# Mixing gated low-rank adapters on eight tiles of the array, and first adapter products in pairs

## The chip, the cores and the metric

The kernel runs on one core of a Trainium2 chip. The core has five instruction streams: TensorE (PE; its weight loads are listed as PEld), VectorE (DVE), ScalarE (ACT), GpSimd (POOL) and SyncE (SP), which here only issues DMAs. Each stream executes its instructions in order and waits on semaphores for the others. The metric is the device time of one execution in microseconds (us); a profiled execution is taken apart from the timed runs and lists every instruction with its start and duration.

## The reference

The input `x` holds 64 rows of 64 channels and 1024 positions. A grouped convolution with nine taps runs along the positions; a condition vector and a bias are added per row and channel. The result goes through a 1024 x 1024 matrix with a bias and through two low-rank adapters ("loras") of rank 32: a shared one, and one that is a gated mixture of sixteen. `x` is added at the end.

```python
out = conv(x, weight, padding=4, groups=4) + (c @ c_weight.T)[:, :, None] + bias   # 64 x 64 x 1024
base_out = out @ kernel + bias
A_eff = einsum("bn,nri->bri", gate, lora_A)        # 8 batches, 16 adapters, rank 32
B_eff = einsum("bn,nor->bor", gate, lora_B)
delta = B_eff (A_eff out)  +  lora_B_shared (lora_A_shared out)
return x + base_out + delta
```

The gate holds one row of sixteen numbers for each of eight batches, and the mixture is computed for any gate.

## The kernel before, in words

**Precision and shape of the work.** Products are made from operands split into a high and a low part: ScalarE rounds the high part (`hi_of`, L264), VectorE or GpSimd subtracts it to get the low part (`lo_of`, L269), and three matmuls (high by high, high by low, low by high) make one product. The 64 rows are worked on as 16 pairs of 256 matrix rows each; eight batches hold two pairs each (`BP = 2`).

**Stages of a pair.** Its input comes in four groups (`xload`). From pair 3 on, a group's convolution is made of two parts: `convo` (the odd positions, three matmuls of 256 columns, fed by `xohi`, `xolo`) and `convd` (the differences, six matmuls, fed by `xdiff`, `xdhi`, `xdlo`). `evmid` (L359) takes the first out of PSUM, on ScalarE in four pieces or on VectorE in one, `evac` (L368) adds it to the second, and `turned` (L382) transposes on VectorE into the tiles `z`. The matrix product follows Strassen's scheme with seven products `prod p j` of twelve 512-column matmuls (L582), whose left sides are blocks of `z` or sums of them (`asum`, `yhi`, `ylo`). Pair 0 is done by the plain scheme (`plain`, L572), while the weights are still being loaded (`wload`), have the shared adapter folded in (`fmm`, `fadd`), and are summed and split (`wsum`, `whi`, `wlo`). Results are put together by `keep`, `xsum`, `ysum`, `radd`, `yadd`, and `total` adds the accumulator to the residual row block (`rload`), which `store` writes out.

**Adapters.** `gmask` (L508) builds the stationary matrix of a mix from the gate. `lload w i` loads raw adapters, sixteen pieces of 256 KB. `mix w j` (L523) multiplies two of them by the gate matrix, `mixout` (L531) copies the PSUM bank out on ScalarE, `mixput` (L538) writes it to a DRAM tile `eff`, from which `aload b` (L548) and `bload b h` (L552) fetch a batch's mixed A and B. `lora p` (L597) is the first adapter product of a pair: sixteen matmuls of 128 columns with a stationary of 32 columns, which go to four column tiles of the array in turn and land in the PSUM tile `axp`. `axlow`, `axsum`, `axhi`, `axlo` sum and split its result; `delta p b` (L655) is the second adapter product, one matmul per block, added to the block's accumulator before `total`. The stationary of `delta` carries two rows of ones; `biput` (L744) writes the high and low part of the bias to the two matching rows of the other operand, `bst`.

**What sets the order.** The string `ORDER` (from L50), called the listing here, names each step with its arguments; a last `v`, `p` or `a` chooses VectorE, GpSimd or ScalarE. The steps are emitted in this order (L748), and each of the five streams is then held to it (L757). Where a step falls against steps of another stream is left to the semaphores. Buffers are few: four `z` tiles (two pairs), five PSUM banks for products and mixes (`pmm`), two for the convolution, four residual blocks.

Of the kernel before, what the change touches and what calls it, by code (L numbers as in the profile page):

```python
# [10 lines left out]
ALU = mybir.AluOpType  # L11
# [39 lines left out]
small 1, warm, twload 1, busy 29, twload 0, cwload, gload, ctload, cwide, cmul, thi 2, small 0, thi 0, tlo 0 v,  # L51
xload 0 0, xhi 0 0, tlo 2 p, xload 0 1, xlo 0 0 v, conv 0 0, twsum v, xhi 0 1, xlo 0 1 v, conv 0 1, sbload 1,
sbhi 1, csum, evac 0 0 v, turned 0 0, xload 0 2, xhi 0 2, xload 0 3, saload 0, sblo 1 p, xlo 0 2 p, evac 0 1 v,
turned 0 1, saload 1, gmask, xhi 0 3, conv 0 2, xlo 0 3 p, sahi 1, conv 0 3, sahi 0, salo 0 v, fmm 0 1,
sbload 0, sbhi 0, fmm 1 1, wload 1 0, evac 0 2 a, xload 1 0, sblo 0 v, fmm 1 0, salo 1 v, xload 1 1, xhi 1 0,
xhi 1 1, xlo 1 1 p, xlo 1 0 v, turned 0 2, yhi 0 0, ylo 0 0 p, wload 0 1, fadd 0 1, evac 0 3 a, fadd 1 0,
conv 1 0, whi 7 0, fmm 4 0, turned 0 3, xload 1 2, xhi 1 2, wlo 7 0 v, fmm 3 0, wload 1 1, conv 1 1, fadd 1 1,
wload 4 0, fmm 0 0, whi 0 1, wload 0 0, fadd 0 0, evac 1 0 a, plain 0 1 0, fadd 4 0, xlo 1 2 p, turned 1 0,
whi 0 0, wlo 0 1 p, fmm 2 1, fmm 2 0, yhi 0 7, evac 1 1 a, conv 1 2, fmm 5 0, wload 2 1, wload 2 0, fadd 2 0,
wlo 0 0 p, plain 0 0 0, xload 1 3, fadd 2 1, wload 5 0, xhi 1 3, fmm 4 1, xlo 1 3 p, plain 0 0 1, whi 0 2,  # L60
ylo 0 7 v, fadd 5 0, plain 0 3 0, whi 7 1, yhi 0 4, wload 3 0, fadd 3 0, whi 0 3, wload 5 1, fmm 3 1, conv 1 3,
turned 1 1, wlo 7 1 v, wload 3 1, xload 2 0, plain 0 1 1, fadd 3 1, whi 7 2, evac 1 2 v, wlo 7 2 p, wload 4 1,
wlo 0 3 p, wlo 0 2 v, lload 0 6, plain 0 2 0, whi 7 3, plain 0 3 1, fadd 4 1, wload 7 1, turned 1 2, whi 1 1,
plain 0 1 2, lload 0 7, xhi 2 0, plain 0 0 2, ylo 0 4 v, plain 0 3 2, xlo 2 0 v, plain 0 2 1, fmm 5 1,
evac 1 3 a, xload 3 0, wlo 7 3 v, plain 0 2 2, turned 1 3, whi 1 0, yhi 0 1, ylo 0 1 v, fadd 5 1, whi 6 1,
conv 2 0, wload 7 0, thi 1, xdiff 3 0 0 v, wload 6 0, evac 2 0 a, lload 1 5, wlo 1 0 p, fmm 7 0, fadd 7 0,
plain 0 2 3, plain 0 0 3, fmm 6 0, lload 0 2, plain 0 3 3, plain 0 1 3, fadd 6 0, lload 0 5, whi 6 0, asum 1 2,
yhi 1 2, lload 0 0, yhi 1 0, plain 0 0 4, plain 0 2 4, wsum 2 2 v, whi 2 2, lload 1 1, wlo 1 1 p, plain 0 0 5,
fmm 6 1, tlo 1 v, plain 0 2 5, rload 0 2, wlo 6 0 v, wsum 2 1 v, wsum 2 3 v, whi 1 2, wlo 1 2 v, plain 0 1 4,
whi 2 1, asum 1 3, whi 1 3, wlo 1 3 p, xload 2 2, wload 6 1, fadd 6 1, xload 2 1, whi 6 2, lload 0 1, xhi 2 2,  # L70
plain 0 3 4, lload 0 4, plain 0 2 6, lload 1 0, lload 0 3, wsum 2 0 v, fmm 7 1, plain 0 2 7, xload 2 3,
plain 0 0 6, fadd 7 1, whi 6 3, total 0 2, lload 1 6, mix 0 0, mixout 0 0 a, wlo 6 2 v, xhi 2 1, wlo 6 3 v,
wlo 6 1 v, wsum 3 2 v, xlo 2 2 v, mix 0 3, mixout 0 3 a, mix 0 2, mixout 0 2 a, wsum 3 0 v, wsum 5 0 v,
mixput 0 0, whi 2 3, mix 0 1, wsum 3 1 v, mix 1 0, mixput 0 3, mixout 0 1 a, xdiff 3 0 1 p, wsum 4 0 v,
conv 2 2, wlo 2 2 v, whi 2 0, wlo 2 0 v, ylo 1 2 v, plain 0 1 5, wsum 5 1 v, rload 0 0, wsum 5 2 v, wsum 4 2 v,
xlo 2 1 v, plain 0 0 7, mixput 0 1, ylo 1 0 p, mixput 0 2, wlo 2 1 v, prod 1 0, plain 0 1 6, wsum 3 3 v,
wsum 5 3 v, rload 0 1, plain 0 3 5, wsum 4 3 v, bihi, whi 3 2, keep 1 0, plain 0 1 7, lload 1 3, wsum 4 1 v,
plain 0 3 6, mixout 1 0 a, lload 1 7, mix 1 3, aload 0, whi 5 3, yhi 1 3, rload 0 3, lload 1 2, ylo 1 3 v,
mixout 1 3 a, total 0 1, lora 0, mix 1 1, turned 2 0, lora 1, whi 5 0, bilo, xohi 3 0, lload 1 4, mix 1 2,
whi 4 2, wlo 4 2 v, mixout 1 1 a, xolo 3 0 v, whi 3 0, wlo 3 0 v, wlo 3 2 v, yhi 1 1, ylo 1 1 v, mixout 1 2 a,  # L80
asum 1 5, total 0 0, whi 4 1, conv 2 1, axlow 1, axsum 1, xload 3 2, wlo 4 1 p, wlo 2 3 v, whi 4 0,
plain 0 3 7, axlow 0, axsum 0, mixput 1 0, mixput 1 3, wlo 4 0 v, xhi 2 3, xlo 2 3 v, wlo 5 3 v, axhi 1,
prod 1 1, biput 0, axlo 1, whi 3 3, asum 1 6, yhi 1 6, wlo 3 3 v, mixput 1 1, evac 2 1 a, turned 2 1, aload 1,
mixput 1 2, total 0 3, evac 2 2 v, turned 2 2, bload 0 0, whi 3 1, axhi 0, prod 1 2, keep 1 2, conv 2 3,
bhi 0 0, biput 1, yhi 2 0, evac 2 3 a, blo 0 0 v, axlo 0, yhi 1 4, bload 0 1, wlo 3 1 p, prod 1 3, ylo 2 0 v,
delta 0 0 1, total 0 0 1, bhi 0 1, blo 0 1 v, ylo 1 6 p, prod 1 6, whi 4 3, delta 0 3 1, wlo 4 3 v, store 0 0,
ylo 1 4 p, turned 2 3, delta 0 2 1, total 0 3 1, xdhi 3 0, convo 3 0, yhi 1 5, whi 5 1, ylo 1 5 v, xdlo 3 0 v,
delta 1 0, total 0 2 1, xload 3 1, keep 1 3, prod 1 4, evmid 3 0 a, store 0 3, xohi 3 1, xdiff 3 1 0 v,
xdiff 3 1 1 p, wlo 5 1 p, delta 0 1 1, total 0 1 1, wlo 5 0 v, xolo 3 1 p, convd 3 0, evac 3 0, turned 3 0,
asum 2 3, rload 1 0, convo 3 1, yhi 2 1, xdhi 3 1, xdlo 3 1 v, prod 2 0, whi 5 2, store 0 2, delta 1 2,  # L90
xload 3 3, keep 2 0, wlo 5 2 p, yhi 2 3, prod 1 5, total 1 0, xohi 3 3, xolo 3 3 v, asum 2 2, xdiff 3 2 0 p,
store 1 0, convo 3 3, evmid 3 1 a, xdiff 3 2 1 p, convd 3 1, ylo 2 3 v, prod 2 3, rload 1 3, delta 1 1,
ylo 2 1 v, xsum 1, asum 2 5, prod 2 1, xdhi 3 2, evac 3 1, turned 3 1, rload 1 2, radd 1 2 v, xdlo 3 2 v,
xdiff 3 3 0 v, delta 1 3, xohi 3 2, xdiff 3 3 1 p, yhi 2 5, xolo 3 2 v, ylo 2 5 p, yhi 2 2, ylo 2 2 v,
evmid 3 3 a, radd 1 3 v, convo 3 2, total 1 2, store 0 1, evmid 3 2 a, convd 3 2, xdhi 3 3, xdlo 3 3 v,
rload 1 1, radd 1 1 v, bload 1 0, lora 2, axlow 2, asum 2 6, prod 2 2, total 1 1, convd 3 3, evac 3 2,
turned 3 2, axsum 2, xload 4 0, xohi 4 0, xolo 4 0 p, bhi 1 0, yhi 2 4, ylo 2 4 v, axhi 2, prod 2 5, keep 2 3,
yhi 3 0, ysum 1 p, xdiff 4 0 0 v, xdiff 4 0 1 v, prod 2 4, store 1 1, xload 4 1, xohi 4 1, xolo 4 1 p,
yadd 1 v, blo 1 0 v, xdhi 4 0, axlo 2, delta 2 0, yhi 2 6, evac 3 3, keep 2 2, xdlo 4 0 v, convo 4 0,
turned 3 3, convd 4 0, rload 2 0, evmid 4 0 a, total 1 3, total 2 0, ylo 3 0 v, lora 3, xdiff 4 1 0 v,  # L100
xdiff 4 1 1 p, asum 3 3, yhi 3 3, prod 3 0, convo 4 1, ylo 3 3 v, evac 4 0, turned 4 0, xdhi 4 1, xload 4 3,
xohi 4 3, xdlo 4 1 v, asum 3 2, xolo 4 3 v, yhi 3 2, ylo 2 6 v, xload 4 2, xdiff 4 2 0 p, store 1 2,
xdiff 4 2 1 p, xohi 4 2, prod 3 3, yhi 3 1, bload 1 1, evmid 4 1 a, delta 2 2, ylo 3 2 v, xolo 4 2 v, asum 3 5,
store 2 0, convd 4 1, xdhi 4 2, xsum 2, convo 4 2, evmid 4 2 a, evac 4 1, xdlo 4 2 v, rload 2 2, radd 2 2 p,
total 2 2, xdiff 4 3 0 v, xdiff 4 3 1 p, prod 2 6, turned 4 1, yhi 3 4, bhi 1 1, convd 4 2, evac 4 2, keep 3 0,
prod 3 2, ylo 3 1 v, rload 2 3, radd 2 3 v, ysum 2 v, convo 4 3, yadd 2 v, xdhi 4 3, xdlo 4 3 v, ylo 3 4 v,
aload 2, prod 3 1, convd 4 3, turned 4 2, blo 1 1 p, xload 5 0, yhi 3 5, xohi 5 0, keep 3 2, asum 3 6,
keep 3 3, xload 5 1, xohi 5 1, delta 2 3, prod 3 4, delta 2 1, xdiff 5 0 0 p, xdiff 5 0 1 v, axlow 3,
ylo 3 5 p, evmid 4 3 a, total 2 3, prod 3 5, store 2 3, xolo 5 0 p, rload 2 1, yhi 3 6, radd 2 1 p, rload 3 0,
axsum 3, evac 4 3, axhi 3, turned 4 3, yhi 4 0, axlo 3, delta 3 0, xload 5 2, xdhi 5 0, store 1 3, xdlo 5 0 v,  # L110
convd 5 0, convo 5 0, ylo 3 6 v, bload 2 0, ylo 4 0 v, xdiff 5 1 0 v, xdiff 5 1 1 p, total 2 1, prod 3 6,
evmid 5 0 a, prod 4 0, asum 4 3, yhi 4 3, evac 5 0, xsum 3, yhi 4 4, ylo 4 3 p, delta 3 3, delta 3 2,
total 3 0, ylo 4 4 v, lora 4, xolo 5 1 p, xdhi 5 1, xdlo 5 1 v, store 3 0, yhi 4 1, ylo 4 1 v, xohi 5 2,
convo 5 1, keep 4 0, bhi 2 0, prod 4 1, rload 3 3, asum 4 2, yhi 4 2, radd 3 3 v, turned 5 0, xdiff 5 2 0 p,
ysum 3 v, evmid 5 1 a, xdiff 5 2 1 v, ylo 4 2 v, delta 3 1, xolo 5 2 p, rload 3 1, radd 3 1 p, blo 2 0 v,
# [702 lines left out]
```

## Time and profile before

| | |
|---|---|
| median of three runs | 448.88 us (448.42 to 450.63) |
| profiled execution, its own time | 447.48 us |
| span of the profile | 445.7 us |
| TensorE, VectorE, ScalarE, GpSimd busy | 98%, 88%, 56%, 53% |
| first matmul of the convolution | 7.47 us after the span's start |
| start of the last matmul | 441.28 us |
| products (L592), convolution (L346), first lora products (L602), mixes (L528) | about 288, 58, 17, 9 us of TensorE |

A row of the order of time gives the start, the duration of one instruction or of a run of like ones, the engine, the line, the operation, output and inputs, their shape and the count. Matmuls overlap: a 512-column matmul is listed with 0.39 us, of which only the first 0.23 separate it from the next one. In the rows of stretches each engine has its busy time and, in brackets, its instructions.

### The profile page before, as it was taken

Reading aid. Unit: us, or ns where it says so; the run is one execution under the profiler, and the core shown is the slowest. Engines: PE = TensorE matmul, PEld = TensorE weight load, DVE = VectorE, ACT = ScalarE, POOL = GpSimd, SP = SyncE. Lnnn points to the kernel's source line nnn. Section 1 sums busy time; section 2 is a strip of 40 time slices with the busy share of each in tenths; the row PEclk is TensorE's granted clock in tenths of the full one; section 3 lists DMA queues with packets and bytes.
Section 4 is the critical chain, followed back from the end, with each engine's and each line's share of the span. In section 5 each row is a group of like instructions: output and inputs, shape, how many; then the busy total and the mean of one; then the engine's idle time right before and its main releaser. Section 6 shows DMA issues by size and latency. Waiting matters only on the chain.

```text
span 445.7 us, 7717 instructions
## 1 busy us (share of the span) xinstructions
PE 438.3 (98%) x2557; PEld 358.7 (80%) x2557; DVE 391.3 (88%) x615; ACT 251.2 (56%) x639; POOL 234.5 (53%) x202
## 2 busy tenths in 40 slices
PE   8999999999999999999999999999999999999996
PEld 7677658888888888888878888888888888888884
DVE  5998979899899899889899899899798989887783
ACT  5877468556655566446555655646554745654440
POOL 3766024754747653555444445464656475467543
PEclk9999999999999999999999999999999999999999
DMA  8999582461625463534345453443536354262243
GB/s 229 300 280 308 147 251 66 142 186 49 186 82 158 136 190 110 170 120 136 97 139 147 151 182 91 119 142 90 175 98 186 95 169 151 72 222 90 91 150 118
DMA packets 52488, 67.05 MB, mean 150 GB/s; under 512 B 6112, under 2 KB 34016, under 8 KB 52448
## 3 DMA queue, kind: packets, MB, share of 16 engines
q1 hardware_dynamic: 42512, 49.83, 38.9%
q10 hardware_dynamic: 9936, 16.73, 10.2%
q8 instruction: 20, 0.33, 0.3%
q14 instruction: 20, 0.16, 0.1%
HBM read 47.65 MB, written 18.87 MB: 149 GB/s over the span
## 4 chain that ended last, share of the span: by engine, by line
PE 91%; DMA 4%; DVE 2%; issue 1%; SPq 0%; ACT 0%; ACTq 0%; DVEq 0%
PE mm_a L592 19%; PE mm_d L592 18%; PE mm_c L592 17%; PE mm_b L592 9%; PE cv L346 8%; PE cm L346 4%; PE axp L602 3%; PE cv L318 2%; DMA wr<-in_dram 2%; PE mx L528 2%; PE mm_a L580 1%; PE mm_c L580 1%; DMA ls<-in_dram 1%; DMA ctt<-in_dram 1%; PE mm_d L580 1%; PE mm_a L660 1%
## 5 line engine op out<-in xcount | busy, mean ns | idle before, releaser
L592 PE MATMUL mm_a<-wh,y 128*128 128x512 f32 x240 | 79.6, 392 | 0.0
L592 PE MATMUL mm_d<-wh,y 128*128 128x512 f32 x240 | 79.2, 391 | 0.0
L592 PE MATMUL mm_c<-wh,y 128*128 128x512 f32 x240 | 79.1, 391 | 0.0
L364 ACT ACTIVATE md<-cm,cadd 128x64 f32<-128x64 f32 x208 | 48.2, 315 | 44.8 <-PE cm L346 41.1
L326 POOL TENSOR_TENSOR xf<-xt 128x256 f32<-128x256 f32 x45 | 33.3, 747 | 49.4 <-DVE xd L270 39.4
L265 ACT CAST xd<-xf 128x512 fp32r<-128x512 f32 x52 | 32.5, 626 | 44.9 <-PE cv L346 20.7
L265 ACT CAST y<-s 128x512 fp32r<-128x512 f32 x60 | 37.2, 624 | 30.5 <-POOL s L412 15.3
L592 PEld LDWEIGHTS mm_a<-wh,y 128*128 128x128 f32 x240 | 45.1, 188 | 9.9 <-issue 0.4
L592 PEld LDWEIGHTS mm_d<-wh,y 128*128 128x128 f32 x240 | 45.1, 188 | 9.2 <-issue 0.2
L592 PEld LDWEIGHTS mm_c<-wh,y 128*128 128x128 f32 x240 | 45.1, 188 | 9.1 <-ACT c L636 0.2
L387 DVE STREAM_TRANSPOSE z<-v 128x512 f32<-128x512 f32 x64 | 45.4, 709 | 3.2 <-PE axp L602 1.9
L592 PE MATMUL mm_a<-wl,y 128*128 128x512 f32 x120 | 46.9, 391 | 0.0
L592 PE MATMUL mm_c<-wl,y 128*128 128x512 f32 x120 | 46.8, 390 | 0.0
L592 PE MATMUL mm_d<-wl,y 128*128 128x512 f32 x120 | 46.8, 390 | 0.0
L346 PE MATMUL cv<-xd,th 128*128 128x256 f32 x208 | 45.7, 282 | 0.4 <-DVE xd L270 0.4
L378 DVE TENSOR_TENSOR v<-cv,md 128x512 f32<-128x512 f32 x52 | 35.7, 686 | 7.7 <-PE cv L346 2.5
L270 DVE TENSOR_TENSOR xd<-xf,xd 128x512 fp32r<-128x512 f32 x41 | 34.5, 842 | 7.6 <-ACT xd L265 7.4
L270 DVE TENSOR_TENSOR y<-s,y 128x512 fp32r<-128x512 f32 x49 | 38.2, 782 | 3.0 <-ACT y L265 2.7
L592 PE MATMUL mm_b<-wh,y 128*128 128x512 f32 x120 | 39.6, 391 | 0.0
L346 PEld LDWEIGHTS cv<-xd,th 128*128 128x128 f32 x208 | 35.5, 188 | 2.4 <-DVE xd L270 0.6
L265 ACT CAST y<-z 128x512 fp32r<-128x512 f32 x49 | 30.6, 625 | 11.8 <-DVE c L641 4.5
L326 DVE TENSOR_TENSOR xf<-xt 128x256 f32<-128x256 f32 x59 | 33.7, 587 | 0.2
(132 smaller groups left out, 1008.2 us busy)
## 6 DMA issues: line engine op xcount, KB each, us to landing
xt<-in_dram SPq DMA_DIRECT2D x64, 258.0 KB, 3.2
r<-in_dram SPq DMA_DIRECT2D x64, 256.0 KB, 3.5
out_dram<-r ACTq DMA_DIRECT2D x63, 256.0 KB, 2.6
ls<-in_dram SPq DMA_DIRECT2D x16, 256.0 KB, 4.6
br<-eff SPq DMA_DIRECT2D x48, 64.0 KB, 2.8
wr<-in_dram SPq DMA_DIRECT2D x16, 176.0 KB, 4.2
eff<-ls SPq DMA_DIRECT2D x16, 128.0 KB, 2.7
wr<-in_dram SPq DMA_DIRECT2D x16, 80.0 KB, 3.9
```

The source lines that it names most:

```text
L265: nc.scalar.copy(dst, src)
L270: engs[eng].tensor_tensor(dst, src, f32(hi), ALU.subtract)
L318: nc.tensor.matmul(ps, a[:, 2 * kt, g, :], b[:, :, kt:kt + P], start=(n == 0), stop=(n == 5))
L326: engs[eng].tensor_tensor(xdf[p, g][:, e], m, odd(p, g), ALU.subtract)
L346: nc.tensor.matmul(ps, a[:, w, g, :], b, start=(n == 0), stop=(n == 2))
L364: nc.scalar.activation(t[:, n], cpm[p, g][:, n], ACTF.Identity, bias=c[:, n:n + 1])
L378: nc.vector.tensor_tensor(v.rearrange("p n (i e) -> p e n i", e=2), cps.pop((p, g)), mid.pop((p, g)).unsqueeze(1).to_broadcast([P, 2, 4, H ...
L387: nc.vector.transpose(z[:, :, :, :, gg, :], vs.pop((p, g)).rearrange("p m j -> p (m j)"))
L528: nc.tensor.matmul(mps[w, j][n * e:n * e + n], gm.rearrange("p b i -> p (b i)"), lraw[w, 2 * j + e], start=True, stop=True)
L580: nc.tensor.matmul(acc[p, BLOCKS[b]], m[:, kk, :], n, start=(k == 0 and q == 0), stop=(k == 7 and q == 2))
L592: nc.tensor.matmul(ps, a[:, k, :], b[bb, k], start=s, stop=(k == HK - 1 and q == 2), skip_group_check=not first)
L602: nc.tensor.matmul(axp[q * R:q * R + R, p % 2, :], a[:, k, :], zs[p, hf][:, k, :], start=k < 2, stop=k >= 6)
```

## The change

It has three parts, and a fourth that goes with them.

1. `mix` works on eight tiles of the array. The gate matrix `gm` has 32 columns instead of 64 and is used in two halves of 64 rows. A mix takes four raw pieces and makes eight matmuls: each piece's upper and lower 64 rows go to a different PSUM bank, and each piece to another quarter of that bank's partitions. There are four mixes instead of eight, each of which fills two banks; copies and stores stay as many (eight, and sixteen of 128 KB), with the order of the numbers in `eff` changed to suit.
2. `loras b` issues the first adapter products of both pairs of a batch one behind the other. In batch 0 the two `lora` steps stay single in the listing; no other TensorE step stands between them.
3. `biput 0` and `biput 1` stand ahead of the stores of the mixed loras, in a row, instead of among them.
4. The whole listing is new: which step comes when on each stream, and which engine takes the low halves, sums and evictions. Eleven `evmid` go from ScalarE to VectorE; of the low halves and differences, some go from GpSimd to VectorE and some the other way.

```diff
-    eff = [dram.tile([NC, NB * GC, AW], F32, tag=f"eff{w}", name=f"eff{w}") for w in range(2)]
+    HI = GC // 2
+    eff = [dram.tile([4, NB, 2, 2, 2, HI, AW], F32, tag=f"eff{w}", name=f"eff{w}") for w in range(2)]
-    gm = const.tile([P, NB, GC], F32, name="gm")
+    gm = const.tile([P, NB, HI], F32, name="gm")
...
     def mix(w, j, pool="m"):
         pl, tag = {"m": (pmm, "mm"), "c": (pcv, "cv")}[pool]
-        mps[w, j] = pl.tile([P, 2 * AW], F32, tag=tag, name=f"mx{w}_{j}")
-        n = NB * GC
-        for e in range(2):
-            nc.tensor.matmul(mps[w, j][n * e:n * e + n], gm.rearrange("p b i -> p (b i)"), lraw[w, 2 * j + e],
-                             start=True, stop=True)
+        for r in range(2):
+            mps[w, j, r] = pl.tile([P, 2 * AW], F32, tag=tag, name=f"mx{w}_{j}_{r}")
+        n, m = NB * HI, P // 2
+        for e in range(4):
+            for r in range(2):
+                nc.tensor.matmul(mps[w, j, r][n * e:n * e + n], gm[m * r:m * r + m].rearrange("p b i -> p (b i)"),
+                                 lraw[w, 2 * e + j][m * r:m * r + m], start=True, stop=True)
...
-    def mixput(w, j):
-        n = NB * GC
-        for e in range(2):
-            dst = eff[w].rearrange("c p a -> p c a")[:, 4 * j + 2 * e:4 * j + 2 * e + 2, :]
-            nc.sync.dma_start(dst, mev[w, j][n * e:n * e + n].rearrange("p (c a) -> p c a", c=2))
+    def mixput(w, j, r):
+        for c in range(2):
+            dst = eff[w][:, :, j, c, r].rearrange("e b i a -> (e b) i a")
+            nc.sync.dma_start(dst, mev[w, j, r][:, c * AW:c * AW + AW])
...
+    def loras(b):
+        for p in range(BP * b, BP * b + BP):
+            lora(p)
```

The listing's TensorE steps from the last plain products to pair 1, before and after (other streams left out):

```
before: mix 0 0, mix 0 3, mix 0 2, mix 0 1, mix 1 0, conv 2 2, plain 0 1 5, plain 0 0 7, prod 1 0,
  plain 0 1 6, plain 0 3 5, plain 0 1 7, plain 0 3 6, mix 1 3, lora 0, mix 1 1, lora 1, mix 1 2,
  conv 2 1, plain 0 3 7, prod 1 1, ...
after:  mix 0 1, plain 0 0 6, plain 0 3 4, mix 0 0, conv 2 2, plain 0 3 5, mix 1 0, plain 0 3 6,
  plain 0 1 5, plain 0 0 7, plain 0 3 7, plain 0 1 6, mix 1 1, plain 0 1 7, conv 2 1, prod 1 0,
  lora 0, lora 1, prod 1 1, ...
```

A batch in the middle, and the end:

```
before: ..., prod 6 5, lora 6, convd 7 3, prod 7 0, prod 6 6, convo 8 0, delta 6 0, prod 6 4,
  convo 8 1, convd 8 0, delta 6 1, delta 6 2, lora 7, prod 7 1, ...
after:  ..., prod 6 5, convo 8 0, prod 7 0, convd 8 0, loras 3, prod 7 1, convo 8 1, prod 6 6,
  convd 8 1, delta 6 1, delta 6 0, delta 6 3, prod 6 4, ...

before: ..., prod 14 6, lora 15, prod 15 0, delta 14 1, prod 15 2, ..., delta 15 2, prod 15 6
after:  ..., prod 14 5, loras 7, prod 14 6, delta 14 0, ..., prod 15 0, ..., delta 15 3, prod 15 6
```

The start of SP's and VectorE's work: before, `twload 1, twload 0, xload 0 0, xload 0 1` with the tap sum `twsum` behind the first input's low half, and `gmask` behind the second transpose; after, `twload 0, xload 0 0, twload 1, xload 0 1` with `gmask` and `twsum` ahead of that low half.

## Prediction

> **What bounds the kernel now.** I read the page first (shares, then the chain that ended last), then stretches of the run side by side, then the matmuls in order of time around the two things that are edited, and last the waits of VectorE.
>
> ```profile
> span 445.7 us, 7717 instructions
> PE 438.3 (98%) x2557; PEld 358.7 (80%) x2557; DVE 391.3 (88%) x615; ACT 251.2 (56%) x639; POOL 234.5 (53%) x202
> ...
> PE 91%; DMA 4%; DVE 2%; issue 1%; SPq 0%; ACT 0%; ACTq 0%; DVEq 0%
> ```
>
> TensorE is busy for 98% of the span and makes 91% of the chain, so its own work sets the end, and VectorE with 88% stands close behind it. The second question is whether that closeness is the same everywhere:
>
> ```profile
> core 0: us, PE busy (x) PEld busy (x) DVE busy (x) ACT busy (x) POOL busy (x), PEclk, DMA share, GB/s
> 0.00:20.00 20.00, 17.54 (x80) 13.74 (x81) 14.94 (x23) 12.87 (x27) 9.73 (x14) 1.00 0.92 257
> 20.00:51.80 31.80, 31.80 (x137) 22.65 (x136) 30.47 (x48) 22.21 (x49) 16.73 (x13) 1.00 0.85 256
> 51.80:137.90 86.10, 85.64 (x515) 68.67 (x514) 77.42 (x120) 52.38 (x131) 44.73 (x38) 1.00 0.49 145
> 137.90:420.00 282.10, 281.67 (x1724) 236.43 (x1726) 253.40 (x407) 158.10 (x421) 150.27 (x130) 1.00 0.44 135
> ```
>
> 51.8 us is the first product of pair 1 (prod 1 0), 137.9 that of pair 4. After 20 us TensorE has hardly an idle slice, and the granted clock is 1.00 in every row. VectorE is at 96% (30.47 of 31.80) before pair 1, at 90% in pairs 1 to 3, and at 90% after them: it keeps up, with little spare.
>
> ```profile
> 56.87 0.39 PE L580 MATMUL mm_b<-wh,y 128*128 128x512 f32 x1
> 57.19 2.24 PE L528 MATMUL mx<-ls,gm 128*64 128x512 f32 x4
> 59.36 1.08 PE L602 MATMUL axp<-z,ar 128*32 128x128 f32 x32
> 60.80 1.08 PE L528 MATMUL mx<-ls,gm 128*64 128x512 f32 x4 [0.35 <-DMA ls<-in_dram]
> 61.81 1.08 PE L602 MATMUL axp<-z,ar 128*32 128x128 f32 x32
> 62.82 1.08 PE L528 MATMUL mx<-ls,gm 128*64 128x512 f32 x4
> 63.83 0.50 PE L318 MATMUL cv<-xs,th 128*128 128x512 f32 x1
> ...
> 97.77 0.28 PE L346 MATMUL cv<-xd,th 128*128 128x256 f32 x1
> 97.97 1.08 PE L602 MATMUL axp<-z,ar 128*32 128x128 f32 x32
> 98.98 0.50 PE L592 MATMUL mm_d<-wh,y 128*128 128x512 f32 x1
> 99.32 0.40 PE L592 MATMUL mm_d<-wl,y 128*128 128x512 f32 x1
> ```
>
> These are the mixes (mx) and first lora products (axp). A 512-column matmul follows the one before it after 0.227 us (12 in 2.72 us), a 256-column one after 0.117. A lora costs more than its 1.01 us (97.97 to 98.98): it begins 0.20 after the last conv matmul where 0.12 was due, so 0.09 lost on entry, and the matmul behind it takes 0.34 instead of 0.23, so 0.11 lost on exit. A visit is 1.21 us.
>
> **The change, part by part.**
>
> *Loras in pairs.* In the mixes two fp32 matmuls of 512 columns side by side take 4.67 / 5 = 0.93 us, so a round is about 0.91 (four times 0.227) with some run-out at the end, and one of 128 columns is a quarter of it, 0.227. A lora's sixteen on four column tiles are four rounds, 0.91 us, which leaves 0.10 of its 1.01 as run-out. Two in a row save one entry (0.09), one exit (0.11) and one run-out (0.10): 2 x 1.21 = 2.42 becomes 2.12. Seven batches times 0.30 = 2.1 us. Loras 0 and 1 also become neighbours on TensorE and are counted with the mixes.
>
> *Mixes.* Before: one run of 20 records from 44.10 to 48.77 (4.67, with entry and exit 4.87), and 57.19 to 63.83 with both loras inside (6.64, with entry and exit 6.83): 11.70 us for eight mixes and two loras, 0.35 us of waiting included. A mix of two matmuls on two column tiles costs 0.93 us there. After: four mixes, each of eight matmuls in tiles of 64 rows by 32 columns. If all eight run together, a mix is again one round of 0.91 plus 0.10, 0.09 and 0.11 = 1.21 us: four are 4.84, the lora pair 2.12, together 6.96. Saved: 4.74 us. No row of this trace shows tiles of half the rows. If the two halves take turns, each mix is 0.91 longer: 4 x 0.91 = 3.64 less saved, 1.1 in all.
>
> Here a rule speaks against the change. The Trainium skill ("TensorE: Matmul & The Clock Gate", Part 3, on what overlaps) says that a weight load overlaps matmuls in flight only when its row group differs. By it the loads of four column tiles on the same rows would stand in line. The row:
>
> ```profile
> L602 PEld LDWEIGHTS axp<-z,ar x512: 106/110/110, 59.4 to 420.3; 128*32 128x32 f32 x171
> ```
>
> A lora has 32 such loads on the same 128 rows, 32 x 0.11 = 3.5 us, and the whole lora takes 1.01: they did overlap. By the rule the mix's 16 loads, eight for each half of the rows, would add up to 8 x 0.11 = 0.88 us to each of four mixes, 3.5 us in all, and the saving falls to 1.2; by the row it stays 4.7. I take the row.
>
> *Around the mix.* It now takes two of five PSUM banks and four raw pieces at once. The copies out stay eight (ScalarE, 0.587 each); between mix 0 1 and mix 0 0 lie two plain steps, 1.37 us, against 2 x 0.587 = 1.17: hidden, and if ScalarE is behind, about 0.6 us each, three times at most. The stores of mixed tiles stay 16 DMAs of 128 KB. In SP's order ten of them stand ahead of the load of batch 0's mixed A, at some 0.62 us an issue; from lload 1 5 on (about 48.6 us) its eight predecessors issue till 53.6, land 2.7 us later, and the load lands after 3.3: 59.6 us, when lora 0 is due at about 59.2. I take 0, bounds 0 to 2. The bias rows go ahead of this on SP, two issues of 0.6 us; biput 1 waits for a tiny VectorE step, and lload 1 5 queues behind it, needed by mix 1 1 some 5 us of products later: nothing, unless VectorE is late.
>
> *The start.* VectorE now does the gate mask and the sum of the tap tables ahead of the first input's low half: 0.68 us later for the third conv matmul. Against it, five folding products instead of three lie among the first convs. 0, bounds -1 and +1.5.
>
> *The new order.* The largest unknown. I added up the listed steps by the mean of their rows (transpose 709 ns, low half of y about 800, block sum 750 on VectorE, one prod 2.72 us on TensorE, and so on), from the listing's head to prod 1 0, from there to prod 4 0, and the rest. VectorE: 52.2, 76.7, 292.4 before; 57.4, 86.3, 275.8 after. TensorE: 45.0, 83.8, 297.7 before; 49.6, 80.6, 291.0 after. The total hardly changes on VectorE (421.3 to 419.5) and GpSimd (236.1 to 242.1), and ScalarE's falls by 10 (eleven mid-tap evictions go to VectorE), but VectorE's work moves forward. Scaled by what the trace measured (45.4 busy for the 52.2, 77.4 for the 76.7), after it is 49.9 and 87.1. TensorE's stretch of pairs 1 to 3 is 80.6 plus the 2.2 that before lost there: 82.8. So VectorE has 4.3 us more work than TensorE there, a share of 105% where before it was 90%. From the start it brings 56.3 - 49.9 = 6.4 us of spare time, of which 5.1 were idle in the first 20 us before anything had landed: 1.3 left. VectorE is late by 3.0 us at pair 4 even if it never idles, by 6.6 at the 96% of the row above. Some of the steps listed there are needed later, which softens it: bounds 0 and 10, and I take 3.5, near the 3.0. Queued behind a late VectorE are the low halves of y and of the conv inputs, for which prod and convd wait, and the transposes, for which the paired loras wait. After pair 4 it has less to do than before (275.8 against 292.4), so nothing is added there.
>
> *The tail.* The last product, two half totals and two half stores stay. The last residual load waits for the store of pair 14's last block, which I put at 6.4 us before the end of the products, against 2.6 + 3.5 us of landings: in time by 0.3. 0, up to +1.5.
>
> **Sum.** -4.74 - 2.10 + 3.5 = -3.3 us on the span of 445.7. The profiled execution took 447.48 by its own time, 1.8 around the span; the median shown, 448.88, is 1.4 above that. I put the difference on the median: 448.9 - 3.3 = 445.5, rounded.
>
> **The rivals.**
>
> *No waits (442.0).* VectorE's forward work is all needed later. For: in the whole of before the waits of TensorE after 20 us are small. 448.9 - 6.8.
>
> *The halves of the array take turns (449.1).* No row speaks for either side; the weight loads above speak for tiles being independent. 445.5 + 3.6; the mixing edit then gains 1.1.
>
> *VectorE becomes the bound in pairs 1 to 3 (452.6, slower).* One mechanism: VectorE cannot run at 105%. At 92% of the time its 87.1 us need 94.7; less 82.8 and the 1.3 spare, TensorE waits 10.6, net +3.8. It cancels the gain when VectorE's share stays at 95.8% (a wait of 6.8), and gives a slowdown above 0.5% under 93.5%. For it: 90% is what before ran at in that stretch. Against: 96% was reached from 20 to 51.8 us with no idle TensorE.
>
> **How the numbers follow.** 0.5%, about what a measurement can tell from no change, is 2.2 us: 446.6 and 451.1. Forecast 0.44, three quarters of it under 446.6; no waits 0.18; turns 0.12, nearly all within; VectorE the bound 0.26, nearly all slower. Faster 0.33 + 0.18 + 0.03 (turns without waits) = 0.54, same 0.20, slower 0.26. The likeliest case alone spans 443 to 448. The range reaches down half-way into "no waits" (441.5) and up to the middle of the slower rival (452.6).
>
> **What would show it.** Mixes: four runs of 16 records, 1.0 us each (1.9 if turns). Loras: seven runs of 64 records in 1.92 us. New waits: idle TensorE between the mixes and pair 4, released by VectorE, about 3.5 us in sum, VectorE's busy share there at 96% or more; after pair 4 no more than before. Wrong would be: waits spread over the later pairs, a start more than 1.5 us later at the first product of pair 1 than the sums say, or a stall at loras 2, 5 or 7, where 2.7 to 4 us of products cover the eviction and the transpose.

## The result and the profile after

The changed kernel takes 454.63 us (median of 4 runs, 453.06 to 454.73), the kernel before, run beside it, 448.65 us (448.07 to 450.63): a ratio of 1.0117, 95% interval 1.0079 to 1.0156 (ratios are of the means of all runs, which lie 5.3 us apart here; the medians lie 6.0 apart). It is slower by 5 to 6 us where 3.3 us of gain were forecast, and lies 2 us above the forecast range. The profiled execution took 454.67 us by its own time, 1.8 around the span, as before.

The page of the kernel after, its shares and its chain:

```profile
span 452.9 us, 7691 instructions
PE 443.2 (98%) x2589; PEld 360.4 (80%) x2589; DVE 391.9 (87%) x615; ACT 241.0 (53%) x595; POOL 241.6 (53%) x213
...
PE 76%; DVE 12%; DMA 5%; ACT 3%; issue 2%; SPq 1%; POOL 0%; ACTq 0%; DVEq 0%; POOLq 0%
```

TensorE still fills 98% of the span, but its share of the chain fell from 91% to 76%, and VectorE's rose from 2% to 12%. Something else is odd: the edits take work from TensorE, and it is busy for 443.2 us instead of 438.3.

The stretches that answer to those of before (columns: length, then the busy time of each engine, the granted clock, DMA; prod 1 0 starts at 59.03 us here, prod 4 0 at 144.91):

```profile
core 0: us, PE busy (x) PEld busy (x) DVE busy (x) ACT busy (x) POOL busy (x), PEclk, DMA share, GB/s
0.00:20.00 20.00, 18.46 (x74) 15.45 (x74) 13.10 (x22) 9.79 (x16) 9.85 (x14) 1.00 0.90 264
20.00:59.03 39.03, 38.83 (x206) 26.47 (x206) 35.54 (x57) 28.48 (x65) 17.32 (x13) 1.00 0.78 240
59.03:144.91 85.88, 84.21 (x511) 68.03 (x511) 80.11 (x130) 49.67 (x124) 45.41 (x38) 1.00 0.45 142
144.91:427.92 283.01, 281.03 (x1716) 234.08 (x1715) 250.13 (x388) 147.67 (x381) 159.87 (x142) 1.00 0.42 131
```

TensorE idles 1.7 us in pairs 1 to 3 and 2.0 after them, where before it idled 0.5 and 0.4. The granted clock is 1.00 in every row, so the clock is not what changed. VectorE's share in pairs 1 to 3 is 93% (80.11 of 85.88).

The two edits themselves, in TensorE's order of time (start, duration):

```profile
45.14 1.09 PE L527 MATMUL mx<-ls,gm 64*32 64x512 f32 x16
47.75 1.09 PE L527 MATMUL mx<-ls,gm 64*32 64x512 f32 x16
51.08 1.09 PE L527 MATMUL mx<-ls,gm 64*32 64x512 f32 x16
55.78 1.09 PE L527 MATMUL mx<-ls,gm 64*32 64x512 f32 x16
...
62.38 1.96 PE L600 MATMUL axp<-z,ar 128*32 128x128 f32 x64 [0.34 <-DMA ar<-eff]
```

Each mix is one run of sixteen, 1.02 us from its first start to the start of the matmul behind it: all eight tiles run together. A pair of loras is one run of 64. Both edits did what they say.

Now the part that the edits don't touch. One product of the kernel before, and one of the kernel after, at the same place in the run:

```profile
200.07 0.39 PE L592 MATMUL mm_c<-wl,y 128*128 128x512 f32 x1
200.75 0.39 PE L592 MATMUL mm_c<-wl,y 128*128 128x512 f32 x1
201.43 0.39 PE L592 MATMUL mm_c<-wl,y 128*128 128x512 f32 x1
```

```profile
200.44 0.40 PE L590 MATMUL mm_a<-wl,y 128*128 128x512 f32 x1
201.14 0.40 PE L590 MATMUL mm_a<-wl,y 128*128 128x512 f32 x1
201.84 0.40 PE L590 MATMUL mm_a<-wl,y 128*128 128x512 f32 x1
```

Between two of these lie three rounds: 0.68 us before, 0.70 after. Over all product and plain rounds the median from start to start is 227 ns before and 233 after, the mean 228.4 and 233.1. The code of a product (prod, plain) is the same in both kernels. It shows in the durations too (minimum, median, maximum in ns), first before, then after:

```profile
L592 PE MATMUL mm_a<-wl,y x120: 387/389/402, 51.9 to 434.4; 128*128 128x512 f32 x120
```

```profile
L590 PE MATMUL mm_a<-wl,y x120: 389/395/403, 59.3 to 441.4; 128*128 128x512 f32 x120
```

With every matmul record of both traces counted from its start to the start of the next (an interval more than 0.05 us over the usual one is a wait; inside and right behind mixes and loras it stays in their rows), the two executions differ by these sums, in us:

| part | before | after | difference |
|---|---|---|---|
| mixes | 8.86 | 4.08 | -4.78 |
| loras | 16.60 | 15.07 | -1.53 |
| 1,355 product and plain rounds | 309.31 | 315.46 | +6.15 |
| all other matmuls | 91.14 | 91.03 | -0.11 |
| waits to 20 us | 2.61 | 2.37 | -0.24 |
| waits from 20 to 60 us | 0.59 | 1.88 | +1.29 |
| waits from 60 to 140 us | 0.88 | 4.26 | +3.38 |
| waits after 140 us | 3.83 | 4.94 | +1.11 |
| first conv matmul | 7.47 | 9.10 | +1.63 |
| from the last matmul's start to the end | 4.40 | 4.67 | +0.27 |
| span | 445.69 | 452.86 | +7.17 |

The first conv matmul waits for loads; in the runs below it came anywhere from 7.2 to 8.5 us, with either order, so the 1.6 us are not counted to the change. What is left is 6.3 us of edits won, 5.5 us of new waits, and 6.2 us of slower rounds. The line between the first two is not sharp: the 0.1 us that is lost on each entry to a mix or a lora, and on each exit, stands among the waits. Counted with the edits, these won about 6.9 us, and the new waits are about 6.1.

### The profile page after: what moved, and what is told of

It is laid out like the page before. It is cut to its first block, busy times and chain, and to the rows that moved or that the text cites. A ratio compares the mean times of both kernels' runs of the same rounds, so it can differ in the third digit from the quotient of the medians.

```text
span 452.9 us, 7691 instructions
## 1 busy us (share of the span) xinstructions
PE 443.2 (98%) x2589; PEld 360.4 (80%) x2589; DVE 391.9 (87%) x615; ACT 241.0 (53%) x595; POOL 241.6 (53%) x213
## 4 chain that ended last, share of the span: by engine, by line
PE 76%; DVE 12%; DMA 5%; ACT 3%; issue 2%; SPq 1%; POOL 0%; ACTq 0%; DVEq 0%; POOLq 0%
PE mm_d L590 17%; PE mm_c L590 15%; PE mm_a L590 12%; PE mm_b L590 9%; PE cv L341 7%; PE cm L341 3%; PE axp L600 3%; DVE y L265 2%; DMA xt<-in_dram 2%; PE cv L313 2%; DVE v L373 1%; PE mm_a L578 1%; PE mm_b L578 1%; PE mm_c L578 1%; DVE r L668 1%
## 5 line engine op out<-in xcount | busy, mean ns | idle before, releaser
L590 PE MATMUL mm_c<-wh,y 128*128 128x512 f32 x240 | 80.6, 397 | 0.6 <-DVE r L668 0.6
L590 PE MATMUL mm_a<-wh,y 128*128 128x512 f32 x240 | 80.7, 397 | 0.2 <-DVE r L668 0.2
L590 PE MATMUL mm_d<-wh,y 128*128 128x512 f32 x240 | 80.2, 396 | 0.0
L321 POOL TENSOR_TENSOR xf<-xt 128x256 f32<-128x256 f32 x57 | 45.1, 800 | 55.6 <-DVE xd L265 48.8
L359 ACT ACTIVATE md<-cm,cadd 128x64 f32<-128x64 f32 x164 | 37.8, 316 | 18.9 <-PE cm L341 16.2
L265 POOL TENSOR_TENSOR xd<-xf,xd 128x512 fp32r<-128x512 f32 x17 | 23.6, 1388 | 43.4 <-ACT xd L260 43.4
L265 DVE TENSOR_TENSOR y<-s,y 128x512 fp32r<-128x512 f32 x54 | 44.6, 828 | 2.1 <-ACT y L260 1.9
L407 POOL TENSOR_TENSOR s<-s,z 128x512 f32<-128x512 f32 x15 | 20.9, 1391 | 32.5 <-DVE y L265 24.9
```

The source lines that it names most:

```text
L265: engs[eng].tensor_tensor(dst, src, f32(hi), ALU.subtract)
L321: engs[eng].tensor_tensor(xdf[p, g][:, e], m, odd(p, g), ALU.subtract)
L359: nc.scalar.activation(t[:, n], cpm[p, g][:, n], ACTF.Identity, bias=c[:, n:n + 1])
L407: engs[eng].tensor_tensor(t, m, n, op)
L590: nc.tensor.matmul(ps, a[:, k, :], b[bb, k], start=s, stop=(k == HK - 1 and q == 2), skip_group_check=not first)
```

## Experiments

### Where in memory the operands lie

Tiles get their places in a partition tag by tag, in the order of their first use in the listing. In the order of before, the conv's split tile (tag xd, 4128 bytes) is used ahead of the first weight piece; then come the pieces (57 times 2048 bytes), v (2048), z (four times 4096) and y. The distance from pieces to y is (57 + 1 + 8) x 2048 bytes, a multiple of 2048. The new order loads the first piece (sbload 1) ahead of the first use of xd (xhi 0 1), so xd comes to lie between pieces and y: (57 + 8) x 2048 + 4128, which is 32 bytes more than a multiple of 2048. The pieces also come to lie 32 bytes off a multiple of 64. Nothing in the diff says so; it follows from two steps that changed places. In a product the piece is the operand that streams, and a 512-byte slice of y is loaded as weights.

The first idea was the start of the streaming operand. Its edits (a_all both, a_gg the first alone):

```diff
-    gg = const.tile([P, NB], F32, name="gg")
+    gg = const.tile([P, 2 * NB], F32, name="gg")[:, 0:NB]
...
-            t = work.tile([P, 2, 4, JB], F32R, tag="xd", name=f"xs{p}_{g}", bufs=1)
+            t = work.tile([P, 8 * JB + 8], F32R, tag="xd", name=f"xs{p}_{g}", bufs=1)
+            t = t[:, 0:8 * JB].rearrange("p (q n j) -> p q n j", q=2, n=4)
```

> The kernel after, with two paddings and nothing else: 32 bytes behind the gate scales (gg, from 32 to 64 bytes) and 32 behind the conv's split tile (xd, 4128 to 4160). All that lies behind them in a partition moves: the 57 weight pieces from 65184 to 65216 (from 32 to 0 modulo 64), the bias and lora B operand bst likewise, while the split activations y stay at 0. Theory (start of the operand that streams through TensorE): in the trace after, every 512-column product round takes 233 ns where before took 227; with the pieces on a multiple of 64 bytes it is 227 again, and 1,356 rounds x 5.5 ns = 7.5 us come back, a little more if bst and the conv operands count too: 446 to 447.5 us, the waits of the trace after (13.5 us over 0.05) staying as they are. Rival (the new order itself, by more VectorE work beside the products or later operands): 233 ns stays and the time is 454 to 455.

> The kernel after with the first padding alone: the pieces (the operand that streams) go to 0 modulo 64 bytes, but the split activations y (the operand that is loaded as weights) go from 0 to 32. Theory, the streaming operand alone counts: product rounds at 227 ns and 446 to 448 us. Rival, any operand of the round off 64 bytes makes it slow: 232 to 233 ns and 454 to 455 us. Rival, the order: the same 454 to 455 us.

The kernel before with 32 bytes put behind xd and behind v (b_w), and with 64 behind gg (b_64):

> The kernel before, its order and all its instructions as they were, with 32 bytes behind the conv's split tile and 32 behind the tile v of the conv's evacuation: the weight pieces move from 69440 to 69472 (from 0 to 32 modulo 64), y from 204608 to 204672 (0 stays 0). Theory (start of the streaming operand): product rounds go from 227 to 232 or 233 ns, 1,356 x 5.5 ns = 7.5 us more, 455 to 457 us. Rival (the slower rounds belong to the new order): 227 ns and 448.6 us, unchanged.

> The kernel before with 64 bytes behind gg, so that everything behind it moves by 64: each operand keeps its place modulo 64 and changes it modulo 128 (the pieces from 64 to 0). Theory (32 off a multiple of 64 is what costs): 227 ns and 448.6 us, as before. Rival (a granule of 128 bytes, or any move): rounds or time differ by over 0.5%.

a_all took 454.12 us, a_gg 453.87, b_w 454.53, b_64 448.75, where before took 449.13 beside them; ratios in the table below. Half of the theory stood: b_w has not one instruction moved, and its rounds went from 227 to 233 ns. Here is its row:

```profile
L594 PE MATMUL mm_a<-wl,y x120: 389/395/397, 53.5 to 441.6; 128*128 128x512 f32 x120
```

So placement alone makes the rounds slow, and the order isn't needed for it. The other half fell: with the pieces on a multiple of 64 the rounds of a_all and a_gg stayed at 233. What set the two fast kernels (before, b_64) apart from the four slow ones was the distance between the operands. That theory was put to four more kernels. a_xd gives xd its old place ahead of the pieces:

```diff
     def sbload(h):
+        if h == 1:
+            work.tile([P, 2, 4, JB], F32R, tag="xd", name="xsp", bufs=1)
         sbr[h] = piece(f"sbr{h}", (DS, HN))
```

> The kernel after, with the conv's split tile (xd) given its place in memory ahead of the weight pieces, where before had it (an unused tile of that tag is laid out when the first piece is); no instruction changes. The pieces go from 65184 to 69312, y stays at 202432: the distance from the pieces to y is again a multiple of 2048 bytes, as in the kernel before (204608 - 69440) and in its copy moved by 64, the two kernels with rounds of 227 ns; in the four with rounds of 233 ns it is 32 or 64 bytes more than one. Theory (distance of the two operands of a round within SBUF): rounds at 227 ns, 7.5 us back, 446 to 447.5 us: below before, since the mixes and loras keep their 6.7 us and the waits (13.5 us against 7.9) take 5.6 of it. Rival (the order's other work keeps the rounds apart, the placement isn't enough): 232 to 233 ns and 454 us.

> As the run a_xd, with 32 bytes behind gg as well: pieces at 69344 and y at 202464, both 32 off a multiple of 64 bytes, the distance a multiple of 2048. Theory, the distance alone counts: 227 ns and the time of a_xd. Rival, the distance counts and each operand has to lie on a multiple of 64 bytes too: 232 to 233 ns and 454 us.

> As the run a_all (pieces at 65216, a multiple of 64), with 64 bytes more behind xd: y at 202560, the distance 128 bytes more than a multiple of 2048. If what counts is the distance modulo 128 or less: 227 ns and 446 to 447.5 us. If modulo more: 232 to 233 ns and 454 us. Since the rounds of one product take weight slices at 0, 512, 1024 and 1536 bytes of y and all are fast in before, the granule should be 512 or less.

> As a_d128 with 128 bytes more: y at 202688, the distance 256 more than a multiple of 2048. If what counts is the distance modulo 256 or less: 227 ns and 446 to 447.5 us; if modulo 512: 232 to 233 ns and 454 us.

All ten kernels, with the places in bytes modulo 256, the median round from start to start, and the time over that of the kernel before (run beside each):

| kernel | pieces | y | distance | round, ns | time, us | ratio (95% interval) |
|---|---|---|---|---|---|---|
| before | 64 | 64 | 0 | 227 | 448.81 (beside a_xd) | 1 |
| b_64 | 128 | 128 | 0 | 227 | 448.75 | 0.9999 (0.9983 to 1.0014) |
| a_xd | 192 | 192 | 0 | 227 | 449.00 | 1.0005 (0.9987 to 1.0023) |
| a_xd32 | 224 | 224 | 0 | 227 | 449.54 | 1.0019 (1.0004 to 1.0035) |
| a_d256 | 192 | 192 | 0 | 227 | 449.29 | 1.0007 (0.9992 to 1.0023) |
| after | 160 | 192 | 32 | 233 | 454.63 | 1.0117 (1.0079 to 1.0156) |
| a_gg | 192 | 224 | 32 | 233 | 453.87 | 1.0104 (1.0084 to 1.0124) |
| b_w | 96 | 128 | 32 | 233 | 454.53 | 1.0121 (1.0104 to 1.0138) |
| a_all | 192 | 0 | 64 | 233 | 454.12 | 1.0113 (1.0089 to 1.0137) |
| a_d128 | 192 | 64 | 128 | 232 | 453.98 | 1.0119 (1.0084 to 1.0154) |

The rows of a_d128, then of a_d256, which differ by 128 bytes of padding and nothing else:

```profile
L591 PE MATMUL mm_a<-wl,y x120: 387/393/404, 58.4 to 440.5; 128*128 128x512 f32 x120
```

```profile
L591 PE MATMUL mm_a<-wl,y x120: 387/389/403, 57.9 to 436.1; 128*128 128x512 f32 x120
```

Every kernel with a distance of 0 modulo 256 is fast, both on and off a multiple of 64 bytes (a_xd, a_xd32); every other one is slow. The distances 32, 64 and 128 were tried; the ones between them weren't. The cost is 5.4 to 5.6 us of this kernel: 454.53 less 449.13 from b_w to before, 454.63 less 449.00 from after to a_xd.

In the matter of time a_xd missed: 449.0 where 446 to 447.5 was expected. In its trace the product rounds are back at 309.41 us, but its waits are 14.8 us where after had 13.5 and before 7.9; 1.3 us more than in after would fit with faster products covering less of VectorE's work. With the rounds put right, the change is level with before. The rest of the loss is in the waits.

### The waits of the new order

The longest waits of TensorE in the kernel after (what waited, on whom, us in total, times, longest):

```profile
PE cv L341 <- DVE v L373: 1.4, 4, 0.5
PE cm L341 <- DVE md L361: 0.6, 2, 0.3
PE mm_c L590 <- DVE r L668: 0.6, 2, 0.3
PE axp L600 <- DMA ar<-eff: 0.3, 1, 0.3
PE mm_b L590 <- DVE r L668: 0.3, 1, 0.3
```

Here v is the evacuation of a conv tile (evac), md that of its middle tap (evmid), r the sum of a product with its residual (total): each frees a PSUM bank that the next conv or product needs. In before that list holds one of this kind, 0.2 us on v. Three things could be behind it: the new mixes, VectorE's load, or the places of the steps. The runs below take them in this order; b_mix_cv, among them, goes back to the rule on placement.

*The old order with the new mixes (b_mix).* The four new mixes stand where the last of their raw pieces lands in the old order; the loras stay single.

```diff
-mix 0 0, mixout 0 0 a, ... mix 0 3, mixout 0 3 a, mix 0 2, mixout 0 2 a, ... mix 0 1, ... mix 1 0,
+mix 0 0, mixout 0 0 0 a, mixout 0 0 1 a, ... mix 0 1 c, mixout 0 1 0 a, mixout 0 1 1 a,
...
-mix 1 3, ... total 0 1, lora 0, mix 1 1, turned 2 0, lora 1, ... mix 1 2,
+total 0 1, mix 1 1, lora 0, turned 2 0, lora 1, ... mix 1 0,
```

> The kernel before with its order of steps and the mixes of the change alone: four mixes of sixteen matmuls in eight tiles instead of eight of two, their evacuations and stores, and the layout of the mixed loras that goes with them; the loras stay one by one. Distance from pieces to y a multiple of 2048 bytes, as in before. Theory (the edits are worth what the prediction's sum says, and the new order is what eats it): mixes in before 8 x 1.46 = 11.7 us, in the traces after 4 x 1.23 = 4.9 us, so 4 to 6.5 us faster where the mixes' neighbours don't wait: 443 to 445 us, with waits of 8 to 9 us. Rival (the mixes lie beside something else that sets the end, so that their time isn't won): 447 to 449 us.

It took 452.5 us, 1.0090 of before (1.0059 to 1.0120): outside of both. (The 11.7 us of the expectation hold loras 0 and 1 as well; the mixes by themselves had 4.8 us to give.) TensorE's order shows why:

```profile
47.82 0.50 PE L313 MATMUL cv<-xsh,th 128*128 128x512 f32 x1 [1.38 <-ACT ls L531]
...
58.92 1.09 PE L525 MATMUL mx<-ls,gm 64*32 64x512 f32 x14 [1.63 <-DVE r L662]
...
78.01 0.47 PE L656 MATMUL dl<-bst,axt 98*128 98x512 f32 x1 [2.15 <-DVE axt L619]
```

A new mix holds two PSUM banks at once. In the old order the second bank comes free only when a residual sum has been read out (1.63 us), a conv waits for the bank that a mix took (1.38), and the first bias and lora product waits for its lora operand (2.15), whose low half stands in VectorE's order behind the mixed B: ScalarE splits that, once it has landed, from 76.13 us on here, in before from 73.06. These 5.2 us are more than the 4.8 that the mixes save. Behind the longest wait comes a second loss. In this row (columns as in the rows of stretches) the granted clock, third from the end, is 0.50:

```profile
79.00:82.40 3.40, 3.40 (x9) 2.63 (x8) 2.33 (x4) 3.13 (x6) 1.16 (x1) 0.50 0.21 82
```

TensorE is busy for these 3.4 us, but its rounds take 0.42 to 0.43 us: 1.7 us lost. The waits alone are enough, though: the three executions of b_mix at a granted clock of 1.00 took 451.6 to 452.4 us. So the edit by itself is no gain in that order as I placed it; what the order costs by itself stays unmeasured.

*The rule for the conv (b_mix_cv).* The same kernel with the conv's operands brought to one place modulo 256:

> The run b_mix with 32 bytes behind gg and the conv's tiles xo enlarged to 2304 bytes, so that xo, xd and the first three pairs' conv tiles lie at the same place modulo 256 as the filters th and tl that are loaded against them (128); pieces and y keep their distance. If the rule found for the products (distance of the two operands modulo 256) holds for the conv's short rounds too: 468 rounds of 256 columns from 117.5 to about 114 ns and 72 of 512 from 235 to 228, 1.5 to 2 us less than b_mix. If it needs long runs of equal rounds (in before the 227 ns come only after three to eight rounds of a product): no difference from b_mix over 0.3%.

It took 455.23 us, 1.0141 of before (1.0104 to 1.0177), its 256-column rounds at medians of 119 to 120 ns where b_mix has 117 to 119, and the granted clock of its profiled run was 0.992, that of b_mix 0.996. No gain for runs of three to six short rounds. Its profiled run is 2.6 us longer than that of b_mix, and two things in the profile add up to that: two stretches at half clock instead of one (1.7 us), and a conv that waits 1.4 us for xsl where it waited 0.5 in b_mix.

```profile
60.30:63.70 3.40, 3.32 (x67) 2.95 (x64) 1.18 (x3) 2.44 (x5) 0.00 (x0) 0.50 0.70 238
80.80:84.10 3.30, 3.30 (x10) 2.55 (x9) 2.77 (x4) 2.88 (x6) 0.94 (x1) 0.50 0.21 79
```

Four of its six executions had a clock of 0.991 or 0.992 and took 455.2 to 457.7 us; the two at 0.996 and 0.999 took 453.2 and 453.0.

*Less work for VectorE (a_xd_ev).* In a_xd every `evmid p g v` becomes `evmid p g a`:

> The run a_xd (order and edits of after, distance as in before) with the eleven evacuations of the conv's middle that the new order puts on VectorE (413 ns each, 4.5 us) on ScalarE, where before has all 64. Theory (VectorE comes late for the conv's tiles and the residual sums, 14.8 us of waits against 7.9): waits 1 to 3 us fewer, 446.5 to 448 us. Rival (what is late is set by the places of the steps in the queues, not by VectorE's load): 448.5 to 449.5 us, or more if ScalarE now releases later.

449.68 us, 1.0020 of before (1.0005 to 1.0035); a_xd was at 449.0. (Before has 52 such steps, all on ScalarE, not 64.) The waits grew from 14.8 to 16.8 us. So this way of taking load off VectorE wins nothing, as the rival had it. But it does not clear VectorE's load. Waits on v and md in a_xd, then in a_xd_ev with two of the new ones:

```profile
PE cv L341 <- DVE v L373: 1.8, 4, 0.7
PE cm L341 <- DVE md L361: 0.7, 2, 0.4
```

```profile
PE cv L341 <- DVE v L373: 0.9, 2, 0.7
PE cm L341 <- ACT md L359: 0.2, 1, 0.2
PE cm L341 <- POOL xo L265: 0.5, 1, 0.5
PE mm_c L592 <- POOL y L265: 0.5, 1, 0.5
```

The waits on v and md shrank, from 2.5 to 1.1 us in these rows, and others came on ScalarE and GpSimd. And between 60 and 140 us, where the prediction had put VectorE's lateness, the run took only 0.7 us off it (74.37 us busy in a_xd, 73.64 here).

*Other places for the steps (a_tun, a_tun2).* Here is one such wait in a_xd, TensorE and VectorE in order of time:

```profile
322.73 1.43 DVE L265 TENSOR_TENSOR xo<-xt,xo 128x256 fp32r<-128x256 f32 x1
323.83 0.39 PE L664 MATMUL mm_c<-bst,axt 98*128 98x512 f32 x1
324.08 0.68 DVE L373 TENSOR_TENSOR v<-cv,md 128x512 f32<-128x512 f32 x1
324.91 0.36 PE L341 MATMUL cv<-xd,th 128*128 128x256 f32 x1 [0.68 <-DVE v L373]
```

The conv (cv) waits for the bank that evac 12 1 (v) empties, and that stands in VectorE's queue behind a low half (xo) which this time takes 1.43 us, where 27 of its kind average 0.58. It could have gone first.

> The run a_xd (new order and edits, distance of pieces to y as in before) with some fifteen steps of the order moved by a few places and nothing else: ahead of six of its longest waits the evacuation or the residual sum that TensorE waits for is put before the VectorE step that it stood behind (evac 8 0 before ylo 7 3, evac 12 1 before xolo 12 3, total 10 0 before turned 12 1 and so on), ahead of four others the next TensorE step that is ready goes first (prod 1 1 before lora 0, loras 1 before prod 2 3), and one conv middle goes to ScalarE. The waits that this touches in the trace of a_xd sum to 6.8 us. Theory (the new order's loss is where its steps stand in the queues): at least half of that comes back, waits 8 to 11.5 us instead of 14.8, 443 to 446.5 us, faster than both kernels. Rival (VectorE's total work or its pauses set these waits, and they come back behind the next step): 13 us or more of waits, 448 to 450 us.

a_tun took 448.14 us, 0.9985 of before (0.9972 to 0.9998). In it prod 1 1 also goes ahead of the copy of pair 1's first product (keep 1 0), so that the copy holds two products instead of one: this kernel's numbers are not the reference's, its work is the same. The expectation missed on the time (it is the rival's), and the trace says which moves failed. From 160 us on, where all moves are VectorE's, the waits fell from 5.3 to 1.9 us (the next expectation has them 0.2 lower). In pairs 1 to 4 the moves on TensorE made new ones of up to 1.3 us, with y, xo and bst late instead; behind two of them this execution, too, has 3.4 us at half clock. The last kernel keeps only the moves on VectorE:

```diff
-yhi 3 4, ylo 3 4 v, blo 1 1 v, xload 5 1, xolo 5 0 p, ylo 3 5 v, prod 3 1, evmid 4 3 v, ... evac 4 3,
+yhi 3 4, ylo 3 4 v, blo 1 1 v, xload 5 1, xolo 5 0 p, evmid 4 3 v, evac 4 3, ylo 3 5 v, prod 3 1, ...
...
-ylo 7 3 v, evac 8 0,
+evac 8 0, ylo 7 3 v,
...
-axlo 7, prod 7 3, evmid 8 2 a, evac 8 1,
+evac 8 1, axlo 7, prod 7 3, evmid 8 2 a,
...
-turned 10 1, yhi 10 0, xdiff 10 3 0 p, total 8 2,
+total 8 2, turned 10 1, yhi 10 0, xdiff 10 3 0 p,
...
-xolo 12 3 v, delta 10 1, ... evac 12 1, turned 12 1, total 10 0,
+evac 12 1, xolo 12 3 v, delta 10 1, ... total 10 0, turned 12 1,
...
-xdiff 13 1 1 v, evac 12 3,
+evac 12 3, xdiff 13 1 1 v,
```

> The run a_xd with eight VectorE steps moved ahead of the step in front of them and no step of another engine: evmid 4 3 and evac 4 3 before ylo 3 5, evac 8 0 before ylo 7 3, evac 8 1 before axlo 7, total 8 2 before turned 10 1, evac 12 1 before xolo 12 3, total 10 0 before turned 12 1, evac 12 3 before xdiff 13 1 1. They are the moves of a_tun whose waits went away there (from 160 us on 5.1 us in a_xd, 1.7 in a_tun, and the 1.0 at 127 us); the moves on TensorE in pairs 1 to 4, behind which a_tun showed new waits of 0.8 to 1.4 us, are left out. Theory (the waits are where the steps stand): 4 us less than a_xd, 444.5 to 446 us, faster than before. Rival (they come back behind the next steps): 448 to 449 us.

It took 444.27 us, 0.9899 of before (0.9878 to 0.9920): faster than both kernels, and 0.2 us below the range of the theory. The same place as above, and the page:

```profile
320.01 0.69 DVE L373 TENSOR_TENSOR v<-cv,md 128x512 f32<-128x512 f32 x1
320.62 0.83 DVE L265 TENSOR_TENSOR xo<-xt,xo 128x256 fp32r<-128x256 f32 x1
321.13 0.40 PE L664 MATMUL mm_c<-bst,axt 98*128 98x512 f32 x1
321.38 0.28 PE L341 MATMUL cv<-xd,th 128*128 128x256 f32 x1
```

```profile
span 442.6 us, 7691 instructions
PE 433.7 (98%) x2589; PEld 358.2 (81%) x2589; DVE 389.1 (88%) x615; ACT 241.4 (55%) x595; POOL 242.7 (55%) x213
...
PE 89%; DVE 4%; DMA 3%; issue 1%; POOL 1%; ACT 1%; SPq 1%; DVEq 0%; ACTq 0%; POOLq 0%
```

The conv follows the delta after 0.25 us, and TensorE is back at 89% of the chain. Waits after 140 us are 1.9 us where a_xd had 5.4, with the same work on VectorE, at the same share of the span (88%). So at least these waits, 3.5 us after 140 us and 1.1 between 60 and 140, were a matter of where eight steps stood. Between 60 and 140 us 4.3 us of waits are left (before has 0.9), the longest on the landing of batch 0's mixed A and on r and md; no run tried these.

## Why the prediction was wrong, step by step

**The step that failed** stands under what bounds the kernel: "A 512-column matmul follows the one before it after 0.227 us (12 in 2.72 us)". The sum took this row of the old trace over to the new kernel without a word, as if it were a property of the instruction. It is one of the instruction and of where its two operands lie, and the new order moved them. Over 1,355 rounds it came to 6.15 us in the trace, and to 5.4 to 5.6 us in the times of b_w and a_xd. No term, bound or rival of the prediction had room for it.

**Mixes, -4.74.** Right. The prediction's sum holds loras 0 and 1 too, with entries and exits: counted so, it is 11.6 us before and 7.0 after (the new wait of lora 0 aside), -4.6. The mixes alone go from 8.86 to 4.08 us, one round per mix, and the halves of the array do not take turns. The rule that was weighed there, on row groups, would have added 0.88 us to each mix; a mix with its sixteen loads takes 1.02 us. The row was the better guide.

**Loras in pairs, -2.10.** About right: with entries and exits, the last fourteen loras take 16.90 us before and 14.57 as seven pairs, -2.33. (The table's -1.53 is all sixteen without entries and exits.)

**Around the mix, 0 with bounds 0 to 2.** Lora 0 did wait for batch 0's mixed A: the profile gives 0.34 us, in a_tun2 1.0. The working had the landing at 59.6 us and lora 0 due at 59.2, so it held a wait of 0.4 already; taking 0 was a slip.

**The new order's waits, +3.5 in pairs 1 to 3.** The size is right where it was put: +3.38 us between 60 and 140 us. The reason is not, so the size was luck. It was VectorE's load: 87.1 us of work, a share of 96% or more; the trace has 80.11 us, 93%. What does set these waits is shown only for the 1.1 us that went when evmid 4 3 and evac 4 3 were moved; for the rest it stays open, since a_xd_ev hardly eased VectorE in that stretch. That "nothing is added there" after pair 4, since VectorE has less to do, was wrong too: +1.1 us after 140 us in the kernel after, +1.5 in a_xd (5.37 less 3.83), and more than 2 us in both once the entries and exits of the loras, 0.2 us a visit and half as many now, are left out. There the reason is shown: moving six steps took 3.5 of these waits in a_xd away, with VectorE's work as it was. A sum of work by stretches can't see an evacuation that stands one step too late. Another 1.3 us came from 20 to 60 us, where the prediction had 0.

**The start and the tail, 0.** The first conv matmul came 1.6 us later in this execution (not counted, as said above), the tail took 0.27 us more.

**The signs of being wrong.** Two of those named came: waits in the later pairs, and prod 1 0 at 59.03 us, 2.7 later than the 56.3 of the sums (1.6 of it is that first conv matmul). No sign named a slower round.

**The rivals.** The time ended on the side of "VectorE becomes the bound", but not by its mechanism: that needed 10.6 us of waits in pairs 1 to 3, and there were 4.3. "No waits" and "turns" are both out.

## What to carry to other kernels

A row of the old trace holds for the new kernel only as far as its surroundings do: when a change reorders the first uses of tiles, compare where the operands of the hottest instruction lie, before any duration is carried over. When a trace is slower everywhere by a few ns a round at full clock, look at placement ahead of the schedule, and test it by moving tiles with padding and no instruction. Sums of busy time tell whether an engine can keep up, not whether the step that frees a bank stands ahead of one that nobody waits for; that is read from the waits, one by one, and a wait whose releaser could have gone first is worth moving.

## What the runs showed of the hardware that was not expected

A 512-column round of these products (fp32r, the rounded operands) whose weights are loaded while the round ahead streams takes 227 ns when streamed operand and weight operand lie a multiple of 256 bytes apart in their partitions, and 232 to 233 ns when they lie 32, 64 or 128 bytes off it; whether each lies on a multiple of 64 bytes makes no difference. The Trainium skill ("TensorE: Matmul & The Clock Gate", Part 2, the step-by-step section) says that the two operands are read through independent ports and that a weight load takes no read bandwidth from the running matmul. By that alone no such difference is due; the ten kernels above show one of 2.5%, and the measurement decides. Why it is so was not tried.

The fast rhythm is not there from the first round on: by place in the product, the mean round of the kernel before is 232 ns for the first, 229 for the third and 227 from the ninth on, and after's stays at 233 all through. That fits with the conv's three to six short rounds having gained nothing from the same placement.

A wait of TensorE can cost more than its length. In the profiled runs of b_mix (once), b_mix_cv (twice) and a_tun (once) the granted clock was 0.50 for 3.4 us, from 0.3 to 1.0 us behind the end of waits of 1.6 to 2.2 us, in a_tun of 0.76 and 0.65 us close together. Each such stretch takes about 1.7 us. Another wait of 1.6 us, in b_mix, was not followed by one; what decides it, these runs don't show.
